# A graph layer's projection dealt out between the tiles of its sums, and counts with one column of weights

## The chip, the cores and the metric

The kernel runs on one core of a Trainium2 chip. The metric is device time in microseconds (us) from launch to end; runs of one kernel agree within about 0.3%. The core's engines are TensorE (PE in the profile, with its weight loads as PEld), VectorE (DVE), ScalarE (ACT), GpSimd (POOL) and SyncE (SP); they run their own instruction streams and wait for one another by semaphores.

## The reference

Two graph convolutions over 6,250 nodes of 256 features and 100,000 edges in eight relations, then a mixture of experts. The edges come sorted by their target dst, and the density of targets falls with dst. Cut to what matters:

```python
def _rgcn_conv(x, W, Wroot, b, src, dst, etype):
    xs = x[src]
    seg = dst * R + etype
    sums = jax.ops.segment_sum(xs, seg, num_segments=N * R)
    cnt = jax.ops.segment_sum(jnp.ones_like(xs[:, 0]), seg, num_segments=N * R)
    mean = sums / jnp.maximum(cnt, 1.0)[:, None]
    mean = mean.reshape(N, R, -1)
    return x @ Wroot + b + jnp.einsum('nrd,rde->ne', mean, W)

h = relu(_rgcn_conv(layernorm(x), W1, Wroot1, b1, src, dst, etype))
x = x + _rgcn_conv(h, W2, Wroot2, b2, src, dst, etype)
# then 8 experts, the best 2 per node: x + sum_e w_e (gelu(ln(x) @ W1[e] + b1[e]) @ W2[e] + b2[e])
```

## The kernel before

Preparation (to about 118 us) normalises x and writes it to DRAM as three bf16 parts per value, whose sum is the f32 value (xs). Then the function `layer` runs twice (the two convolutions), and then the expert stage.

The 100,000 edges are 782 *tiles* of 128 edges. `_plan` joins neighbouring tiles into 194 *groups* of one to six tiles, so that all targets of a group lie in a window of at most 64 nodes. It deals the groups out in one sequence, `seq`, from both ends of the edge list towards a block near the middle; one group is one *step* q. The nodes are 49 *blocks* of 128. `whole[b]` is the step after whose group no edge of block b is left, by an estimate with a margin `dev` (L167).

For a group, `tiles_in` (L668) does three things. ACT writes zeros into a window of sums `pg` in PSUM (L672; two buffers, so a group's zeros wait for the sum of the group two before it to be taken out). GpSimd issues one indirect DMA per tile, which fetches the 128 source rows into a buffer `ge` (L680, 13 buffers). DVE makes a one-hot matrix `oh` per tile (L686). `sums` (L691) then runs on TensorE: per tile six matmuls with the gathered rows as weights (two halves of the features by three bf16 parts) and `oh` as the moving operand (L696); in layer 0 a seventh with a 128 x 128 matrix of ones as weights (L699), which counts the edges into the third slice of `pg`. `add` (L702) lets DVE add the window to a ring in SBUF that holds the sums of three blocks (L710); there are two rings, for the two ends.

When a block is whole, a few functions finish it. `counts` (L751) fetches the counts of its nodes by an SP DMA from partition 0 of the ring (cn, L760), `invert` (L763) transposes them and takes reciprocals. `project` (L770) runs nine products on TensorE, the node's own features with Wroot and the eight relations' sums with W (L783: 36 passes of 256 columns in f32), two at a time into a PSUM buffer `pr` (two buffers), and DVE gathers them into `h` with the reciprocals (L791, L793). `clear` (L797) lets ACT zero the block's slots in the ring (L800). `finish` (L803) writes the block's rows to DRAM, by SP; in layer 0 after relu and a split into three bf16 parts (L808 to L815), in layer 1 with a layernorm besides. `turn` (L824) transposes the block on TensorE for its next use (L830, L314). `logits` (L835) works out the gate of the experts, and for every few blocks picks the experts (`choose`) and appends the nodes to the experts' lists (`append`, one block per step, eight SP DMAs, L423).

The table `due` (L848) says how many steps after `whole[b]` each of them is emitted: root -1, counts 0, invert 1, project, clear and finish 2, turn 3, logits 4. In step q the loop (L866) emits the next group's `tiles_in`, then project and clear, turn, finish, then this group's `sums`, invert and logits, then `add`, root and counts. A scheduler then sets the final order on each engine from the dependencies and its own costs, so that the emitted order is a wish. Engines issue in that final order.

Ring slots are shared, so `_plan` also gives each group `bounds` (L171 to L177): the first and last block that its window may touch. They are worked out from the steps at which blocks are read (`read`, with READ = 2) and cleared (`taken`, with TAKE = 3), and are checked against the data on the chip before the layers run; data that break them take another, slower path. Adds and projections have no semaphores between them where the bounds part them; an add waits for the clears that are due before its step.

Of the kernel before, what the change touches and what calls it, by code (L numbers as in the profile page):

```python
# [48 lines left out]
P = 128  # L49
# [45 lines left out]
Z = 4.8  # L95
WIN = 64
RB = 3
READ = 2
TAKE = 3
EARLY = 30  # L100

# [1 line left out]
def _plan(N, E, R):  # L103

    T = -(-E // P)

    def windows(ts, n):

        mid = n // 2
        lo, hi = [0] * n, [-(1 << 30)] * n
        for t in ts:
            for k in range(n + 1):
                i0, i1 = t * P, max(0, t + k - mid) * P
                mean = N * (i1 * i1 - i0 * i0) / (E * E)
                sd = 2 * N * i0 / (E * E) * math.sqrt(abs(i1 - i0)) + 0.004 * abs(mean)
                if k < n:
                    lo[k] = min(lo[k] if t != ts[0] else 1 << 30, math.floor(mean - Z * sd) - (k < mid))
                if k:  # L120
                    hi[k - 1] = max(hi[k - 1], math.ceil(mean + Z * sd) + (1 if k <= mid else 2))
        shift = -min(lo)
        w = [(a + shift, b + shift) for a, b in zip(lo, hi)]
        return shift, w, max(b for _, b in w)


    NB = -(-N // P)
    mid = max(0, round((N / 4 - P / 2) / P))
    split = round(T * math.sqrt((mid + 0.5) * P / N))
    regions = []  # L130
    t = 0
    while t < T:
        left = (split if t < split else T) - t
        for n in range(min(6, left), 0, -1):
            ng = max(1, min(36, left) // n)
            shift, w, width = windows((t + n // 2, t + n * (ng - 1) + n // 2), n)
            if width <= WIN:
                break
        regions.append((t, n, ng, shift, w, width))
        t += n * ng  # L140
    groups = []
    for r, (t0, n, ng, *_) in enumerate(regions):
        for g in range(ng):
            groups.append((t0 + g * n, n, r))
    NG = len(groups)
    up = [g for g in range(NG) if groups[g][0] < split]
    down = list(range(NG - 1, len(up) - 1, -1))
    size = [sum(groups[g][1] for g in s) for s in (up, down)]
    seq, at, n = [], [0, 0], [0, 0]
    while len(seq) < NG:  # L150

        s = int(n[1] * (size[0] - EARLY) < n[0] * size[1])
        if at[s] == len((up, down)[s]):
            s = 1 - s
        g = (up, down)[s][at[s]]
        seq.append(g)
        at[s] += 1
        n[s] += groups[g][1]
    step = {g: q for q, g in enumerate(seq)}

    whole = []
    for b in range(NB):
        if b == mid:
            whole.append(NG - 1)
            continue
        p = math.sqrt((b + 1 if b < mid else b) * P / N)
        dev = Z * math.sqrt(E * p * (1 - p)) + 1  # L167
        t = int(min(E - 1, E * p + dev) // P) if b < mid else int((E * p - dev) // P)
        whole.append(step[next(g for g, (t0, n, _) in enumerate(groups) if t0 + n > t)])


    bounds = []
    for g in range(NG):
        read, taken = ([b for b in range(NB) if whole[b] + n < step[g]] for n in (READ - 1, TAKE))
        if g < len(up):
            bounds.append((sum(b < mid for b in read) or -NB, sum(b < mid for b in taken) + RB))
        else:  # L177
            n = sum(b > mid for b in read)
            bounds.append((NB - sum(b > mid for b in taken) - RB, NB - n if n else 2 * NB))
    return T, regions, groups, seq, len(up), mid, whole, bounds  # L180
# [3 lines left out]
def kernel(  # L184
# [20 lines left out]
    nc = tc.nc  # L205
    N, D = x.shape
    E = src.shape[0]
    R = gW1.shape[0]
    X = fW1.shape[0]
    H = fW1.shape[2]  # L210
    KD = D // P
    KH = H // P
    NB = -(-N // P)
# [28 lines left out]
    ones16 = const.tile([P, P], BF16, name="ones16")  # L242
# [84 lines left out]
    T, regions, groups, seq, UP, mid, whole, bounds = _plan(N, E, R)  # L327
    assert T == C
    NG = len(groups)
# [306 lines left out]
    with tc.If(go == 1) as cmp:  # L636
        with ExitStack() as arm:
# [9 lines left out]
            step = {g: q for q, g in enumerate(seq)}  # L647
# [8 lines left out]
            def layer(k):  # L656
# [34 lines left out]
                def sums(g):  # L691
                    pg, got = state[g]
                    for ge, oh, m, a, b in got:
                        for c in range(KD):
                            for s in range(3):
                                nc.tensor.matmul(pg[:, c, :, a:b], ge[:m, s, c, :], oh, start=False, stop=False,  # L696
                                                 skip_group_check=True)
                        if nd > KD:
                            nc.tensor.matmul(pg[:, KD, :, a:b], ones16[:m], oh, start=False, stop=False,  # L699
                                             skip_group_check=True)  # L700

                def add(g):  # L702
                    pg, _ = state.pop(g)
# [59 lines left out]
                def invert(b):  # L763
                    if k == 0:
# [2 lines left out]
                        nc.vector.tensor_scalar(invs[:, b], pc[:, :R], 1.0, None, op0=OP.max)  # L767
                        nc.vector.reciprocal(invs[:, b], invs[:, b])

                def project(b):  # L770

                    n = rows(b)
                    xT = state.pop(("x", b))
                    s0 = (b % RB) * P
                    ring = of(b)
                    h = ap.tile([P, D], F32, name="h", bufs=2)
                    lhs = [(R, [xT[:, c, :n] for c in range(KD)])]
                    lhs += [(r, [ring[:, c, r, s0 : s0 + n] for c in range(KD)]) for r in range(R)]
                    for i in range(0, R + 1, 2):
                        pr = psum.tile([P, 2, D], F32, name="pr", tag="mm", bufs=MM)  # L780
                        for j, (r, chunks) in enumerate(lhs[i : i + 2]):
                            for c in range(KD):
                                mm = nc.tensor.matmul(pr[:n, j], chunks[c], w[:, c, r, :], start=(c == 0), stop=(c == KD - 1))  # L783
                                if r < R:
                                    for a in adds[int(b > mid)][state["adds", b] :]:
                                        tc.declare_no_dep(of_block(b, mm), a, reason="bounds")
                                    tc.add_manual_dep(mm.ins, state["whole", b].name, wait, reason="whole")
                        for j, (r, _) in enumerate(lhs[i : i + 2]):
                            if r == R:
                                extra = bias1 if k == 0 else state.pop(("xb", b))  # L790
                                nc.vector.tensor_tensor(h[:n], pr[:n, j], extra[:n], OP.add)  # L791
                            else:
                                nc.vector.scalar_tensor_tensor(h[:n], pr[:n, j], invs[:n, b, r : r + 1], h[:n],  # L793
                                                               op0=OP.mult, op1=OP.add)
                    state["h", b] = h

                def clear(b):  # L797
# [47 lines left out]
                tiles_in(seq[0])  # L845
                due = {}
                for b, q in enumerate(whole):
                    for d, f in ((-1, root), (0, counts), (1, invert), (2, project), (2, clear), (2, finish), (3, turn), (4, logits)):  # L848
                        due.setdefault(q + d, []).append((f, b))

                todo = []
# [8 lines left out]
                def run(q, *fs):  # L860
                    for f, b in due.get(q, []):
                        if f in fs:
                            f(b)

                cleared[:] = [[(-1, ins) for _, ins in c] for c in cleared]
                for q in range(NG + 5):  # L866
                    if k == 1 and q == 2:

                        with tc.issue_after(state["zeroed"].ins):
                            load_gnn_weights(gW2, None, None, nc.scalar, gw)  # L870
                    batch()
                    if q + 1 < NG:
                        tiles_in(seq[q + 1])
                    if q == 0 and k == 0:
                        for c in range(KD + 1):
                            nc.vector.memset(rings[0][:, c], 0.0)
                            nc.scalar.copy(rings[1][:, c], zeros[:, None, 0:1].to_broadcast([P, R, RING + WIN]))
                    run(q, project, clear)
                    run(q, turn)
                    run(q, finish)  # L880
                    if q < NG:
                        sums(seq[q])
                    run(q, invert, logits)
                    if q < NG:
                        add(seq[q])
                    run(q, root, counts, join)
# [6 lines left out]
    with cmp.Else():  # L893
        with ExitStack() as arm:
# [35 lines left out]
            with tc.tile_pool(name="sortp", bufs=1, side="right") as sp:  # L930
# [22 lines left out]
                for d in range(NB):  # L953
                    oh = sp.tile([P, C], F32, name="oh", bufs=2)
# [319 lines left out]
```

## Time and profile before

| | |
|---|---|
| median of 10 runs | 3026.54 us (3020.66 to 3031.13) |
| the profiled execution | 3027.49 us, span 3025.7 us |
| mean granted TensorE clock | 0.927 |
| gathers of layer 0, first to last start | 81.9 to 1121.2 us |
| gathers of layer 1, first to last start | 1162.2 to 2160.6 us |
| expert stage's first weight DMA | 2219.2 us |
| DVE ring adds, L710 | x388, 1176 ns, 456.3 us |
| ACT zeroing of pg, L672 | x388, 981 ns, 380.0 us |
| ACT clearing of the ring, L800 | x98, 2325 ns, 227.8 us |

A row of the profile names line, engine, operation, output and inputs, the count, then busy time, mean ns of one, and the idle time of the engine just before, with what ended it. In rows in order of time, the first number is the start in us from the span's start, the second the time in us. A stretch's row has its length, then the busy time of PE, PEld, DVE, ACT and POOL with the number of instructions, then the granted clock, the DMA share and GB/s. A wait's row has the total in us, how often, and the longest. Matmuls are pipelined: an instruction's duration (240 ns) is its latency, and successors start far closer.

### The profile page before, as it was taken

To read this page: it belongs to the slowest core of one execution; us is meant where nothing else is said; L and a number is where in the kernel's file an instruction comes from. 1 tells how busy PE (TensorE), PEld (TensorE's weight loads), DVE (VectorE), ACT (ScalarE), POOL (GpSimd) and SP (SyncE) were. 2 spreads that over 40 slices of the span, in tenths; PEclk is the share of its full clock that TensorE was granted. 3 is DMA by queue.
4 is the path that set the end of the run, shared out by engine and by line. 5 is a ranking of instruction groups with operands and counts; after the bars stand their busy time and mean duration, and the time that the engine had idled before them with its cause. 6 is when DMAs were issued, how large, how long until landed. Compare 5 with 4: busy or idle time off the path is not lost.

```text
span 3025.7 us, 52037 instructions
## 1 busy us (share of the span) xinstructions
PE 2553.5 (84%) x18131; PEld 2157.9 (71%) x18131; DVE 1620.6 (54%) x4676; ACT 1018.8 (34%) x1378; POOL 1811.2 (60%) x2109
## 2 busy tenths in 40 slices
PE   5578888888888876888888888898839999999997
PEld 2466776776777765666766767777728888888886
DVE  7566676766666674666766776676711111111111
ACT  6334444434343442333323323233312222222221
POOL 1767777777777764777777777777413333333332
PEclk9789999999999997989989998999969999999999
DMA  7555565656555554666566666666364444444441
GB/s 259 149 144 161 166 173 164 173 157 170 162 171 165 167 142 132 176 176 176 169 174 176 174 177 169 175 180 173 111 200 117 109 117 107 108 122 107 107 120 20
DMA packets 215591, 461.05 MB, mean 152 GB/s; under 512 B 50716, under 2 KB 123222, under 8 KB 215190
## 3 DMA queue, kind: packets, MB, share of 16 engines
q0 software_dynamic: 120384, 334.45, 41.6%
q1 hardware_dynamic: 83724, 112.33, 11.2%
q10 hardware_dynamic: 11210, 10.81, 1.2%
q8 instruction: 149, 2.44, 0.3%
q14 instruction: 124, 1.02, 0.1%
HBM read 412.02 MB, written 46.31 MB: 151 GB/s over the span
## 4 chain that ended last, share of the span: by engine, by line
PE 63%; DMA 20%; ACT 5%; DVE 5%; issue 4%; POOL 1%; SPq 0%; DVEq 0%; ACTq 0%; POOLq 0%
PE pr L783 25%; DMA ge<-xs,idx 15%; PE ph L1214 12%; PE po L1225 12%; PE pg L696 11%; ACT ring L800 2%; DVE ring L710 2%; ACT pg L672 1%; DMA cn<-ring 1%; POOL ge L680 1%; DMA xt<-in_x_dram 1%; ACT xt L496 1%; PE pt L1198 1%; PE pg L699 1%; DMA fw<-in_L_ffn_W_dram 1%
## 5 line engine op out<-in xcount | busy, mean ns | idle before, releaser
L680 POOL DMA_INDIRECT ge<-xs,idx x1564 | 1522.0, 973 | 622.1 <-issue 224.4
L696 PE MATMUL pg<-oh,ge 128*128 128x200 bf16 (+24 forms) x9384 | 827.1, 240 | 321.5 <-DMA ge<-xs,idx 227.4
L696 PEld LDWEIGHTS <-ge 128*128 128x128 bf16 x9384 | 669.8, 104 | 443.6 <-DMA ge<-xs,idx 279.9
L783 PE MATMUL pr<-gw,ring 128*128 128x256 f32 (+1 forms) x3136 | 753.0, 395 | 2.1 <-DVE h L793 1.8
L783 PEld LDWEIGHTS pr<-gw,ring 128*128 128x128 f32 (+1 forms) x3136 | 615.9, 199 | 99.0 <-DVE h L793 5.8
L710 DVE TENSOR_TENSOR ring<-pg,ring 128x1176 f32 (+31 forms) x388 | 456.3, 1176 | 279.4 <-PE pg L696 136.1
L672 ACT COPY pg<-zeros 128x1176 f32<-128x1176 f32 (+31 forms) x388 | 380.0, 981 | 528.0 <-DVE ring L710 505.3
L793 DVE SCALAR_TENSOR_TENSOR h<-pr,invs,h 128x256 f32<-128x256 f32 (+1 forms) x784 | 376.4, 480 | 165.4 <-PE pr L783 148.5
L800 ACT COPY ring<-zeros 128x3072 f32<-128x3072 f32 (+1 forms) x98 | 227.8, 2325 | 686.1 <-PE pr L783 625.5
L1215 ACT ACTIVATE hT<-ph,bcol 128x256 f32<-128x256 f32 x424 | 200.8, 474 | 534.5 <-PE ph L1214 534.5
L1214 PE MATMUL ph<-xT,w 128*128 128x256 f32 x1696 | 378.3, 382 | 0.0
L1225 PE MATMUL po<-fw,hT 128*128 x1696 | 374.4, 379 | 0.0
L1225 PEld LDWEIGHTS po<-fw,hT 128*128 128x128 f32 x1696 | 322.2, 190 | 43.8
L1214 PEld LDWEIGHTS ph<-xT,w 128*128 128x128 f32 x1696 | 321.0, 192 | 42.2
L686 DVE TENSOR_SCALAR oh<-iota,rel 128x152 bf16<-128x152 f16 (+25 forms) x1564 | 335.4, 274 | 19.6 <-PE pg L699 14.6
L1186 POOL DMA_INDIRECT xg<-xnd,ti x106 | 105.6, 996 | 350.0 <-DMA ti<-tlist 236.0
L1230 POOL DMA_INDIRECT out_dram<-fo,ti x106 | 168.7, 1591 | 230.2 <-DVE wt L1199 116.3
L1228 DVE TENSOR_TENSOR fo<-po,b2b 128x256 f32<-128x256 f32 x106 | 45.0, 425 | 299.4 <-PE po L1225 299.4
L699 PE MATMUL pg<-oh,ones 128*128 128x128 bf16 (+24 forms) x782 | 187.8, 240 | 0.0
L1209 DVE COPY bcol<-b1c 128x8 f32 x53 | 9.0, 171 | 302.4 <-ACT hT L1215 301.9
L699 PEld LDWEIGHTS <-ones 128*128 128x128 bf16 x782 | 82.3, 105 | 2.6
L783 PE MATMUL pr<-gw,hTs 128*128 128x256 f32 (+1 forms) x196 | 70.9, 485 | 2.3 <-ACT hTs L831 2.1
(190 smaller groups left out, 1345.2 us busy)
## 6 DMA issues: line engine op xcount, KB each, us to landing
w<-in_L_ffn_W_dram SPq DMA_DIRECT2D x53, 1024.0 KB
ge<-xs,idx POOLq DMA_INDIRECT x1564
xt<-in_x_dram SPq DMA_DIRECT2D x96, 128.0 KB
xs<-xb SPq DMA_DIRECT2D x8, 1152.0 KB
xs<-hb SPq DMA_DIRECT2D x48, 192.0 KB
fw<-in_L_ffn_W_dram ACTq DMA_DIRECT2D x8, 1024.0 KB
xt<-in_x_dram SPq DMA_DIRECT2D x8, 768.0 KB
out_dram<-h SPq DMA_DIRECT2D x48, 128.0 KB
```

Of the source, the lines that this page charges most:

```text
L672: state["zeroed"] = nc.scalar.copy(pg[:, :nd, :, :wd], zeros[:, None, None, :wd].to_broadcast([P, nd, R, wd]))
L680: nc.gpsimd.indirect_dma_start(out=ge[:m].rearrange("p s k d -> p (s k d)"), out_offset=None, in_=xs[k][:, :], in_offset=bass.IndirectOffs ...
L686: nc.vector.tensor_scalar(oh, iota16[:m].rearrange("p (r d) -> p r d", r=R)[:, :, a:b], rel[:m, t : t + 1], None, op0=OP.is_equal)
L696: nc.tensor.matmul(pg[:, c, :, a:b], ge[:m, s, c, :], oh, start=False, stop=False, skip_group_check=True)
L699: nc.tensor.matmul(pg[:, KD, :, a:b], ones16[:m], oh, start=False, stop=False, skip_group_check=True)
L710: a = nc.vector.tensor_tensor(slot, pg[:, :nd, :, :wd], slot, OP.add).ins
L783: mm = nc.tensor.matmul(pr[:n, j], chunks[c], w[:, c, r, :], start=(c == 0), stop=(c == KD - 1))
L793: nc.vector.scalar_tensor_tensor(h[:n], pr[:n, j], invs[:n, b, r : r + 1], h[:n], op0=OP.mult, op1=OP.add)
L800: ins = nc.scalar.copy(at, zeros[:, None, None, 0:1].to_broadcast([P, nd, R, P]))
L1214: nc.tensor.matmul(ph[:, :TK], w1[:, k, h * P : (h + 1) * P], xT[:, k, :], start=(k == 0), stop=(k == KD - 1))
L1215: nc.scalar.activation(hT[:, h, :], ph[:, :TK], AF.Gelu, bias=bcol[:, h : h + 1], scale=1.0)
L1225: nc.tensor.matmul(po[:, :D], hT[:, k, f * P : (f + 1) * P], rhs, start=(k == 0), stop=(k == KH - 1))
```

## The change

`project` no longer issues its nine products. It makes a function `pair` for each two of them and puts them into a list, `pairs`. `sums` takes one from the list after each tile (`go_on`), and what is left follows the group's last tile. Within a step, turn and clear now come first, then finish, project, `sums` with the pairs, the leftover pairs, and the rest as before. Clear, finish, turn and logits are due one step later, and there is one step more at the end. The counts matmul loads one column of the ones and writes partition 0 alone; the other partitions of the third slice keep the zeros. `READ` is gone, `read` is worked out without the extra step, and the margin `dev` grows from 1 to 32 edges.

```diff
-        dev = Z * math.sqrt(E * p * (1 - p)) + 1
+        dev = Z * math.sqrt(E * p * (1 - p)) + P / 4
...
-        read, taken = ([b for b in range(NB) if whole[b] + n < step[g]] for n in (READ - 1, TAKE))
+        read, taken = ([b for b in range(NB) if whole[b] + n < step[g]] for n in (0, TAKE))
...
-                            nc.tensor.matmul(pg[:, KD, :, a:b], ones16[:m], oh, start=False, stop=False,
+                            nc.tensor.matmul(pg[0:1, KD, :, a:b], ones16[:m, 0:1], oh, start=False, stop=False,
                                              skip_group_check=True)
+                        go_on()
...
+                pairs = []
+
+                def go_on():
+
+                    if pairs:
+                        f, i = pairs.pop(0)
+                        f(i)
...
-                    for i in range(0, R + 1, 2):
+                    def pair(i):
                         pr = psum.tile([P, 2, D], F32, name="pr", tag="mm", bufs=MM)
...
+                    pairs.extend((pair, i) for i in range(0, R + 1, 2))
                     state["h", b] = h
...
-                    for d, f in ((-1, root), (0, counts), (1, invert), (2, project), (2, clear), (2, finish), (3, turn), (4, logits)):
+                    for d, f in ((-1, root), (0, counts), (1, invert), (2, project), (3, clear), (3, finish), (4, turn), (5, logits)):
...
-                for q in range(NG + 5):
+                for q in range(NG + 6):
...
-                    run(q, project, clear)
-                    run(q, turn)
+                    run(q, turn, clear)
                     run(q, finish)
+                    run(q, project)
                     if q < NG:
                         sums(seq[q])
+                    while pairs:
+                        go_on()
```

More of the change, by code (lines that the diff above doesn't have):

```diff
@@ L97 @@
 RB = 3
-READ = 2
 TAKE = 3
```

## The prediction

> **What bounds the kernel now.** I read the page's engine sums first, then the costliest groups, then GpSimd's rows in order of time, then TensorE's waits.
>
> The page's engines and groups:
>
> ```profile
> span 3025.7 us, 52037 instructions
> ...
> PE 2553.5 (84%) x18131; PEld 2157.9 (71%) x18131; DVE 1620.6 (54%) x4676; ACT 1018.8 (34%) x1378; POOL 1811.2 (60%) x2109
> ...
> L680 POOL DMA_INDIRECT ge<-xs,idx x1564 | 1522.0, 973 | 622.1 <-issue 224.4
> L696 PE MATMUL pg<-oh,ge 128*128 128x200 bf16 (+24 forms) x9384 | 827.1, 240 | 321.5 <-DMA ge<-xs,idx 227.4
> ...
> L783 PE MATMUL pr<-gw,ring 128*128 128x256 f32 (+1 forms) x3136 | 753.0, 395 | 2.1 <-DVE h L793 1.8
> ...
> L699 PE MATMUL pg<-oh,ones 128*128 128x128 bf16 (+24 forms) x782 | 187.8, 240 | 0.0
> ```
>
> POOL's 60% hides a saturated engine, because the expert stage (from 2219 us on) hardly uses it. GpSimd's rows in order of time show it:
>
> ```profile
> 652.75 0.95 POOL L680 DMA_INDIRECT ge<-xs,idx  x1 [0.30 <-issue]
> 654.00 0.94 POOL L680 DMA_INDIRECT ge<-xs,idx  x1 [0.30 <-issue]
> ...
> 660.80 0.95 POOL L680 DMA_INDIRECT ge<-xs,idx  x1 [5.86 <-PE pg L696]
> 662.05 0.94 POOL L680 DMA_INDIRECT ge<-xs,idx  x1 [0.30 <-PE pt L830]
> ```
>
> Each gather is followed by 0.30 us whatever the releaser named; 1,541 of the 1,563 gaps are 0.3 us. Gathers run from 81.9 to 1122.2 us in layer 0 and from 1162.2 to 2161.6 in layer 1. What the longer gaps have over 0.31 us sums to 34 us in layer 0 and 7 in layer 1; the one at the layer change is 40. So issuing alone needs 1040 - 34 = 1006 us in layer 0 (1.29 per tile) and 992 in layer 1. Nothing that only helps TensorE can win more than the 41 us in which GpSimd waited for one of 13 buffers. TensorE over layer 0's sums (88 to 1129 us), by stretch and by waits:
>
> ```profile
> 88.00:1129.00 1041.00, 861.35 (x7389) 737.41 (x7385) 702.76 (x1669) 435.31 (x481) 762.98 (x778) 0.92 0.58 163
> ...
> PE pg L696 <- DMA ge<-xs,idx: 80.4, 103, 3.9
> PE pg L696 <- ACT pg L672: 66.7, 62, 5.6
> PE pt L830 <- DVE h L808: 15.9, 13, 3.9
> PE pc L766 <- DMA cn<-ring: 10.1, 14, 2.1
> ```
>
> TensorE is second in line: 861 us busy. About 207 busy stretches end in a wait, and each counts a matmul's tail (0.24 long, while its successor would start 0.07 after it): 35 us. Its own need is 826. The parts agree: 782 tiles at 0.48 (the mean of 471 undisturbed cycles of seven matmuls) are 375, 49 blocks of 36 projection passes at 0.231 are 408, transposes about 40.
>
> **The counts (L699).** One matmul per tile of layer 0, 782 of them, keeps its moving columns and loads one weight column instead of 128. Before, it costs only its streaming: L696 to L699 to L696 runs without a break (1126.00, next at 1126.07). Narrow weights do occur in this trace: L411 loads eight columns, L383 one. L411 between the same sums:
>
> ```profile
> 1541.99 0.22 PE L411 MATMUL rpl<-rcol,rnum 128*8 128x128 bf16 x1
> 1542.14 0.34 PE L696 MATMUL pg<-oh,ge 128*128 128x176 bf16 x2
> 1542.41 0.22 PE L411 MATMUL rpl<-rcol,rnum 128*8 128x128 bf16 x1
> ...
> 1543.73 0.22 PE L411 MATMUL rpl<-rcol,rnum 128*8 128x128 bf16 x1
> 1543.88 0.25 PE L696 MATMUL pg<-oh,ge 128*128 128x176 bf16 x1
> 1544.06 0.22 PE L411 MATMUL rpl<-rcol,rnum 128*8 128x128 bf16 x1
> ```
>
> From L411 to L411 with one 176-column matmul between is 0.33 us; streamed at the usual pace (0.057 for L411's 128 columns, 0.078 for 176) it would be 0.135. With two between: 0.42 against 0.21. So a narrow matmul costs about 0.20 us more: its load isn't started under the matmul ahead, nor the next wide load under it. For one column, L381 to L383 takes 0.11 where L380 to L381 takes 0.03, and the second L383 to the next sum about 0.10: some 0.16 more. The load rows read 80 ns for one column and about 100 for 128. Bounds: -0.02 x 782 = -16 us, if only the load's duration mattered, to 0.25 x 782 = 196. I take 0.18, between the two measured forms, since L383 has the weights and L411 the length and the neighbours of the new count: **+141 us of TensorE in layer 0**, none in layer 1 (no counts there).
>
> The Trainium skill ("TensorE: Matmul & The Clock Gate", LDWEIGHTS) has load time grow with the number of columns; by that alone one column saves nearly 0.1 us of loading per tile, and by estimate 83 us of loads would go. The same page's "Weight-path perf modes" reserves its fast load for exactly 128 columns of a type other than FP32, which speaks against this change. The rows of L383 and L411 side with the second: loads barely shorter, and a gap on both sides.
>
> **The projection dealt out (L779 to 796, pairs run from `sums`).** The 36 passes and eight DVE accumulations of a block stay the same. Emitted whole, a project of 36 passes holds TensorE about 8 us while GpSimd issues 6 gathers; the 5.86 us stall above follows two projects 4 us apart. Afterwards each tile's buffer comes free at least as early. The compiled order of the changed kernel keeps part of the lumps: of 882 projection matmuls per layer, those in runs of 16 or more without a tile between fall from 484 to 194 (layer 0) and from 531 to 140 (layer 1). Switching costs a little: the load of an f32 pass is 0.19 us and a bf16 matmul ahead hides half of it, so 0.1 each; runs of projection rise from 86 to 137 in layer 0 (+5 us) and from 93 to 189 in layer 1 (+10, in idle time). A run behind a narrow count pays 0.09 more (L411, two f32 passes, L411: 0.78 us against 0.49, less the 0.20): 137 x 0.09 = +12.
>
> **Clear, finish, turn and logits a step later; bounds.** Clear (L800, 2.3 us on ACT, 98 times) no longer sits in ACT's queue behind a project; it waited 625 us there, which cost TensorE little. Turn comes a step after finish, so the 16 us of TensorE waiting for L808 go. Clear stands nearer to the add that needs its slots (DVE waited 6.7 us for it in 10 cases); if every block waits 1 us, 98 us of DVE queue, which is hidden while buffers are free. The SP DMAs of finish are the same in number, a step later, and nobody reads them before the layer ends. I worked the plan's new bounds through with the reference's dst: the ring arm is still the one taken. The wider `dev` moves two of 49 blocks by one group. NG + 6 steps add one empty step.
>
> **Tail.** The compiled order puts the three-block choice behind the next-to-last project, so at the end one more list append comes after the last project. An append cycle is 4.6 to 5.2 us (L415 at 2199.40, 2204.60, DVE free at 2209.2); it partly overlaps: **+2**, between 0 and +5. The gap at the layer change stays: the same adds, cn DMA and two projects; 0.
>
> **Sum.** Layer 0, TensorE: 826 + 141 + 5 + 12 = 984 us of own need, against GpSimd's 1006. With the servers this close, the waits decide. ACT's zeroing (62 times, 1.08 us and 0.17 of tail) shrinks as a three-tile group now takes 0.6 us longer: 62 x 0.65 = 40. cn stays: 12. Of the waits for gathers (103 x 0.95 = 98) I keep a quarter, since a queue of 13 buffers between equal servers still runs dry at the start and after stalls: 25. 984 + 77 = 1061 against 1041: **+20**. Layer 1: TensorE keeps its slack, of 7 us of stall 5 go: **-5**. Tail **+2**. Total +17 on the profiled execution's 3027.49, which stands 0.95 above the median of the ten: 3043.5, say **3044 us**.
>
> **Rivals.**
> - *Smoothing wins.* If a count costs under about 0.1 us more, TensorE's need stays below 930 and GpSimd's stalls mostly go: -34 and -5 of them at best, less what is left of early stalls (14 us by 240 us, at a granted clock of 0.85): about 3000, at the very best 2988. For it: buffers do come free earlier, layer 1's lumps shrink most, and a TensorE that idles less may hold a higher granted clock (0.92 over layer 0; f32 passes average 0.231 us, 0.216 undisturbed), worth up to 0.06 x 826 = 50 us of need. Against it: the L411 rows. The sign flips where 826 + 17 + 77 + 782 times the count's extra comes to 1044 (1041 and the 3 us that layer 1 and the tail give back): at 0.16 us, which is the value of the one-column rows; below it the kernel is faster.
> - *Nothing measurable (within 0.2%, 6 us, about what a measurement of this kernel can tell).* Counts between 0.15 and 0.17 us extra, or a clock gain that pays for dearer ones.
> - *Much slower.* Counts at 0.25 (+55) with ACT's waits unshrunk (+37, because clear now falls between the zeroings): 3044 + 55 + 37 = 3136, or 3081 to 3099 with one of them.
>
> **Numbers.** Slower by TensorE's need 0.56 (much slower within that: 0.12), nothing 0.14, faster 0.30. Range 2999 to 3092: it leaves out the best of the smoothing case and the far end of the much slower one. Within the forecast's own case: 3033 to 3092.
>
> **What would show it.** Gaps of about 0.1 us on both sides of each count, tile cycles of about 0.65 in place of 0.48; TensorE busy near 95% in layer 0 with its waits for gathers down from 80 us to some 25; GpSimd's long gaps (PE pg) growing in layer 0 to over 50 us and almost none in layer 1; the wait for L808 gone. The forecast is wrong if tile cycles stay near 0.5, or if TensorE's clock rises enough to pay for the counts.

## The result, and the profile after

The changed kernel takes 3055.74 us (median of 11 runs, 3039.96 to 3063.01), the kernel before 3023.87 (39 runs, 3013.04 to 3033.20). The ratio is 1.0103, with an interval of 1.0090 to 1.0116: slower by 32 us or 1.0%, where 17 us were forecast. The profiled execution took 3058.49 us, its span is 3056.7, 31.0 more than before. By the starts of GpSimd's gathers, these 31 us lie as follows:

| us | before | after | difference |
|---|---|---|---|
| up to the first gather | 81.9 | 83.4 | +1.6 |
| layer 0, first to last gather | 1039.3 | 1068.6 | +29.3 |
| of it, gaps of GpSimd beyond 0.31 us | 34.4 | 65.8 | +31.4 |
| layer change, last to first gather | 41.0 | 41.2 | +0.2 |
| layer 1, first to last gather | 998.4 | 994.4 | -4.0 |
| of it, gaps beyond 0.31 us | 7.2 | 2.5 | -4.8 |
| after the last gather | 865.1 | 869.0 | +3.9 |

So the loss is layer 0's, the only layer that counts edges, and there it is time that GpSimd waits for a buffer. The page of the changed kernel, its engines and groups:

```profile
span 3056.7 us, 52032 instructions
...
PE 2674.8 (88%) x18131; PEld 2151.1 (70%) x18131; DVE 1618.0 (53%) x4676; ACT 1015.3 (33%) x1378; POOL 1809.4 (59%) x2110
...
L679 POOL DMA_INDIRECT ge<-xs,idx x1564 | 1520.5, 972 | 650.7 <-PE pg L695 231.7
L695 PE MATMUL pg<-oh,ge 128*128 128x200 bf16 (+24 forms) x9384 | 907.2, 243 | 238.7 <-DMA ge<-xs,idx 143.6
...
L791 PE MATMUL pr<-gw,ring 128*128 128x256 f32 (+1 forms) x3136 | 766.8, 392 | 2.7 <-DVE h L801 2.7
...
L698 PE MATMUL pg<-oh,ones 128*1 128x128 bf16 (+24 forms) x782 | 180.9, 231 | 0.0
...
L698 PEld LDWEIGHTS <-ones 128*1 128x1 bf16 x782 | 62.1, 79 | 107.0 <-issue 58.8
```

The counts' own row (L698) looks cheaper than before, 180.9 us against 187.8, and their load takes 79 ns. TensorE's sum is 121 us higher all the same. The largest part of GpSimd's idle time (231.7 of 650.7 us, which include the 0.30 us behind every gather) is now put down to `PE pg L695`, the matmuls that free a gather's buffer. Where the 121 us come from is seen only in TensorE's rows in order of time. Here are the same tiles at the full clock, 192 and 272 columns wide, first in the kernel before, then in the changed kernel:

```profile
308.33 0.66 PE L696 MATMUL pg<-oh,ge 128*128 128x192 bf16 x6
308.83 0.25 PE L699 MATMUL pg<-oh,ones 128*128 128x192 bf16 x1
308.91 0.70 PE L696 MATMUL pg<-oh,ge 128*128 128x192 bf16 x6
309.44 0.26 PE L699 MATMUL pg<-oh,ones 128*128 128x192 bf16 x1
309.53 0.86 PE L696 MATMUL pg<-oh,ge 128*128 128x272 bf16 x6
```

```profile
329.22 0.67 PE L695 MATMUL pg<-oh,ge 128*128 128x192 bf16 x6
329.82 0.24 PE L698 MATMUL pg<-oh,ones 128*1 128x192 bf16 x1
330.00 0.71 PE L695 MATMUL pg<-oh,ge 128*128 128x192 bf16 x6
330.64 0.25 PE L698 MATMUL pg<-oh,ones 128*1 128x192 bf16 x1
330.82 0.87 PE L695 MATMUL pg<-oh,ge 128*128 128x272 bf16 x6
```

From one tile's first sum to the next tile's it was 0.58 and 0.62 us, and is 0.78 and 0.82. Over 521 cycles of seven matmuls without a gap above 0.15 us the mean is 0.674 us, over 494 such cycles before it was 0.479; this mixes widths and granted clocks. At one width (medians) the extra is nearly the same everywhere: 0.19 at 24 columns, 0.20 at 152, 0.20 at 256. About half of it lies behind the count (0.16 us to the next sum in place of 0.08) and half ahead of it. At 0.19 us, 782 of these make 149 us. The two stretches of the changed kernel (layer 0's sums, layer 1's) and TensorE's waits in layer 0:

```profile
88.00:1160.00 1072.00, 979.77 (x7380) 729.49 (x7380) 704.17 (x1665) 434.19 (x477) 761.96 (x779) 0.93 0.56 158
1193.00:2190.00 997.00, 835.44 (x6739) 691.03 (x6740) 665.54 (x2177) 298.17 (x364) 754.89 (x782) 0.91 0.62 176
```

```profile
PE pg L695 <- ACT pg L671: 57.2, 56, 5.4
PE pg L695 <- DMA ge<-xs,idx: 34.9, 25, 16.1
PE pc L766 <- DMA cn<-ring: 10.4, 15, 1.8
PE pt L839 <- DVE h L817: 2.0, 3, 1.0
```

The longest wait for a gather, 16.1 us, is the one ahead of the layer's first matmul. It stood in the kernel before as well, where it ended ahead of the window of the waits, which starts at 88 us (before, then after):

```profile
86.64 0.32 PE L696 MATMUL pg<-oh,ge 128*128 128x40 bf16 x4 [16.12 <-DMA ge<-xs,idx]
```

```profile
88.20 0.28 PE L695 MATMUL pg<-oh,ge 128*128 128x40 bf16 x3 [16.13 <-DMA ge<-xs,idx]
```

TensorE is busy 980 of 1072 us (91%, 83% before). Without that first one, its waits for gathers fell from 80 us in 103 cases to 19 us in 24, the wait for `h` from 16 to 2; the wait for ACT's zeros only from 67 to 57. GpSimd shows the other side:

```profile
490.74 0.94 POOL L679 DMA_INDIRECT ge<-xs,idx  x1 [1.76 <-PE pg L695]
491.99 0.94 POOL L679 DMA_INDIRECT ge<-xs,idx  x1 [0.30 <-issue]
499.30 0.94 POOL L679 DMA_INDIRECT ge<-xs,idx  x1 [6.37 <-PE pg L695]
500.54 0.94 POOL L679 DMA_INDIRECT ge<-xs,idx  x1 [0.30 <-PE pg L695]
```

Gaps over 0.33 us grew from 17 to 42 in layer 0 and fell from 4 to 2 in layer 1. Of their 66 us 52 lie before 500 us, where 17 of 34 lay in the kernel before: all of the loss. From 88 to 400 us the granted clock fell, though TensorE was busier. The stretches from 200 to 300 and from 300 to 400 us, before and after:

```profile
200.00:300.00 100.00, 83.70 (x723) 72.55 (x724) 67.49 (x172) 41.56 (x48) 73.18 (x77) 0.91 0.58 164
300.00:400.00 100.00, 80.83 (x752) 69.90 (x750) 67.89 (x162) 45.00 (x50) 74.98 (x79) 0.93 0.60 168
```

```profile
200.00:300.00 100.00, 86.45 (x625) 63.53 (x624) 63.27 (x149) 38.04 (x43) 63.29 (x65) 0.85 0.49 138
300.00:400.00 100.00, 90.63 (x671) 65.66 (x670) 60.63 (x150) 35.82 (x39) 70.19 (x73) 0.88 0.56 158
```

The clock's record knows two values in this layer, 1.0 and 0.5. Of these 200 us, 31 ran at 0.5 before and 53 after, and at 0.5 a tile's cycle of 200 columns takes 1.21 us before and 1.41 after (medians of 3 and 9), where GpSimd issues a gather every 1.25 us. How much of the loss comes by way of the clock is not shown.

### The profile page after: what moved, and what is told of

Same layout as the page of the kernel before. It is cut to its first block, busy times and chain, and to the rows that moved or that the text cites. A ratio compares the mean times of both kernels' runs of the same rounds, so it can differ in the third digit from the quotient of the medians.

```text
span 3056.7 us, 52032 instructions
## 1 busy us (share of the span) xinstructions
PE 2674.8 (88%) x18131; PEld 2151.1 (70%) x18131; DVE 1618.0 (53%) x4676; ACT 1015.3 (33%) x1378; POOL 1809.4 (59%) x2110
## 4 chain that ended last, share of the span: by engine, by line
PE 70%; DMA 14%; ACT 5%; DVE 5%; issue 4%; POOL 1%; SPq 0%; DVEq 0%; ACTq 0%; POOLq 0%
PE pr L791 25%; PE pg L695 15%; PE ph L1225 12%; PE po L1236 12%; DMA ge<-xs,idx 9%; PE pg L698 3%; DVE ring L710 2%; ACT pg L671 2%; ACT ring L809 1%; POOL ge L679 1%; DMA xt<-in_x_dram 1%; DMA cn<-ring 1%; PE pt L1209 1%; PE pt L313 1%; PE pl L322 1%
## 5 line engine op out<-in xcount | busy, mean ns | idle before, releaser
L679 POOL DMA_INDIRECT ge<-xs,idx x1564 | 1520.5, 972 | 650.7 <-PE pg L695 231.7
L695 PE MATMUL pg<-oh,ge 128*128 128x200 bf16 (+24 forms) x9384 | 907.2, 243 | 238.7 <-DMA ge<-xs,idx 143.6
L695 PEld LDWEIGHTS <-ge 128*128 128x128 bf16 x9384 | 664.9, 105 | 399.0 <-DMA ge<-xs,idx 175.2
L791 PE MATMUL pr<-gw,ring 128*128 128x256 f32 (+1 forms) x3136 | 766.8, 392 | 2.7 <-DVE h L801 2.7
L791 PEld LDWEIGHTS pr<-gw,ring 128*128 128x128 f32 (+1 forms) x3136 | 591.8, 195 | 87.2 <-DVE h L801 4.3
L710 DVE TENSOR_TENSOR ring<-pg,ring 128x1464 f32 (+30 forms) x388 | 456.6, 1177 | 284.6 <-PE pg L695 128.1
L698 PE MATMUL pg<-oh,ones 128*1 128x128 bf16 (+24 forms) x782 | 180.9, 231 | 0.0
L698 PEld LDWEIGHTS <-ones 128*1 128x1 bf16 x782 | 62.1, 79 | 107.0 <-issue 58.8
L315 ACT COPY tT<-pt 128x256 f32<-128x256 f32 (+1 forms) x98 | 36.2, 370 | 147.1 <-PE pt L313 129.8
```

The lines of the kernel that those rows point to most:

```text
L679: nc.gpsimd.indirect_dma_start(out=ge[:m].rearrange("p s k d -> p (s k d)"), out_offset=None, in_=xs[k][:, :], in_offset=bass.IndirectOffs ...
L698: nc.tensor.matmul(pg[0:1, KD, :, a:b], ones16[:m, 0:1], oh, start=False, stop=False, skip_group_check=True)
L710: a = nc.vector.tensor_tensor(slot, pg[:, :nd, :, :wd], slot, OP.add).ins
```

## The experiments

The theory: the dealt-out order takes lumps away and costs nothing; the narrow counts cost TensorE 0.19 us each; and in layer 0, where TensorE and GpSimd are nearly level, part of that comes back as waits of GpSimd. The rival: the order itself costs (dealt-out pairs, later steps), and the counts are hidden.

The chips were not alike: on the two that the first eleven runs fell on the kernel before takes 3793 to 3833 us, on that of the last run 3024, and every ratio is to the kernel before beside it on the same chip.

| run | kernel | us | kernel before there | ratio |
|---|---|---|---|---|
| e1_wide_counts | dealt out, counts of 128 columns | 3697.66 | 3832.76 | 0.9643 (0.9604 to 0.9681) |
| e2_narrow_only | kernel before, narrow counts | 3838.41 | 3832.76 | 0.9998 (0.9971 to 1.0024) |
| e3_wide_undealt | later steps, not dealt out, 128 columns | 3834.63 | 3832.76 | 1.0006 (0.9988 to 1.0024) |
| e4_counts_last | dealt out, narrow counts in one run per group | 3703.51 | 3832.76 | 0.9669 (0.9629 to 0.9709) |
| r2_changed | the changed kernel | 3671.54 | 3793.36 | 0.9680 (0.9645 to 0.9714) |
| r2_wide_counts | as e1 | 3668.36 | 3793.36 | 0.9667 (0.9642 to 0.9693) |
| r2_narrow_only | as e2 | 3803.02 | 3793.36 | 1.0021 (1.0002 to 1.0040) |
| l1_light_before | kernel before, a third of the gathered bytes | 3827.94 | 3798.28 | 1.0085 (1.0053 to 1.0117) |
| l2_light_changed | changed kernel, a third of the gathered bytes | 3713.04 | 3798.28 | 0.9793 (0.9753 to 0.9833) |
| l3_light_wide | as e1, a third of the gathered bytes | 3700.42 | 3798.28 | 0.9746 (0.9714 to 0.9778) |
| r3_wide_counts | as e1 | 3660.45 | 3798.28 | 0.9632 (0.9603 to 0.9661) |
| n1_counts_twice | the changed kernel, each narrow count twice | 3186.29 | 3023.75 | 1.0541 (1.0517 to 1.0565) |

### One part at a time

Wide counts in the changed kernel:

```diff
-                            nc.tensor.matmul(pg[0:1, KD, :, a:b], ones16[:m, 0:1], oh, start=False, stop=False,
+                            nc.tensor.matmul(pg[:, KD, :, a:b], ones16[:m], oh, start=False, stop=False,
```

> The changed kernel with the counts' weights 128 columns wide again; the order on every engine stays that of the changed kernel. Theory (the narrow load costs 0.19 us per tile and makes TensorE a second bound of layer 0): the tile cycle returns from 0.63 to 0.45 us at the median, GpSimd's waits for buffers in layer 0 fall from 66 us to under 20, the time to about 3000 us (2990 to 3012), faster than before. Rival (the order is what costs: pairs between tiles, clear and finish a step later): within 12 us of the changed kernel, 3044 or more.

The same lines the other way round in the kernel before (narrow counts alone):

> The kernel before with the counts' weights one column wide, and nothing else. Theory: TensorE needs some 145 us more in layer 0, and with whole projects of 8 us GpSimd waits for buffers more than the 66 us of the changed kernel: 3060 to 3090 us. Rival (the order is what costs): 3024 us, like the kernel before.

Wide counts, and the changed kernel's list of pairs emptied where `project` stands, so that only the later steps and bounds of the change are left:

```diff
                     run(q, project)
+                    while pairs:
+                        go_on()
                     if q < NG:
                         sums(seq[q])
```

> Wide counts, and each block's five pairs issued together ahead of the group's sums; clear, finish, turn and logits stay a step later. Theory (buffers come free earlier because pairs stand between tiles): most of the gain of the wide dealt kernel is missing, 3010 to 3026 us, and GpSimd still waits over 25 us in layer 0. Rival (ACT's and TensorE's waits were the cause, and the later clear and turn are what helps): within 6 us of the dealt kernel with wide counts.

Narrow counts, all of a group's in one run behind its sums:

```diff
+                        go_on()
+                    for ge, oh, m, a, b in got:
                         if nd > KD:
                             nc.tensor.matmul(pg[0:1, KD, :, a:b], ones16[:m, 0:1], oh, start=False, stop=False,
                                              skip_group_check=True)
-                        go_on()
```

> The changed kernel with its one-column counts issued in one run at the end of each group, 196 runs instead of 782. Theory (what costs is the change between narrow and wide weights, once per run): 196 x 0.19 = 37 us of TensorE instead of 149, GpSimd's waits in layer 0 under 30 us, 3000 to 3018 us. Rival (each narrow matmul costs by itself, by its load or by its write to one partition): as the changed kernel, 3045 to 3060 us.

Measured: 0.9643, 0.9998, 1.0006 and 0.9669. On this chip dealing the pairs out gains all of 3.3 to 3.6%; later steps and bounds alone (e3) and narrow counts alone (e2) do nothing that can be told from zero. Two expectations missed. One is the level: the kernel before took 3833 us there, so no forecast in microseconds holds. The other is the theory's for e2, which was to be 1.012 to 1.022 of the kernel before and is 0.9998, as its rival had it. A gain larger than all of GpSimd's waits in the first profile (41 us) could only come from waits that the first profile doesn't have, so the changed kernel itself had to be run on such a chip.

### The changed kernel on a slower chip

No edit: the changed kernel, and e1 and e2 again.

> The changed kernel once more, as the reference point of this call. Where gathers land as fast as in the first profiles (kernel before about 3024 us), 1.010 of the kernel before. Where the kernel before takes about 3830 us and most of TensorE's waiting is for late gathers, dealing out should win whatever the counts cost: 0.965 to 0.975.

> Wide counts, dealt out. Theory (narrow counts cost TensorE 149 us in layer 0, and that matters where GpSimd's issue is the only other bound): where the kernel before takes about 3024 us, 0.988 to 0.996 of it, with GpSimd's waits for buffers in layer 0 under 20 us and a tile cycle of 0.45 us at the median. Rival (the order is what costs): within 0.4% of the changed kernel. Where the kernel before takes 3830 us, 0.964 again.

> The kernel before with narrow counts only. Theory: where the kernel before takes about 3024 us, 1.012 to 1.025 of it, with GpSimd's waits in layer 0 over 66 us, because whole projects and dearer tiles add up. Rival (counts are harmless): 1.000. Where the kernel before takes 3830 us, 1.000 again.

All three are near what was expected for a chip of this kind: 0.9680 (0.965 to 0.975), 0.9667 (0.964) and 1.0021 (1.000). The change that costs 1.0% on the first chip gains 3.2% here. The stretches of layer 0 and layer 1 tell why the counts don't matter here. First the changed kernel, then the one with wide counts:

```profile
88.00:1430.00 1342.00, 1065.62 (x7271) 768.49 (x7272) 691.42 (x1645) 431.15 (x472) 748.44 (x775) 0.84 0.44 126
1490.00:2780.00 1290.00, 904.62 (x6582) 735.63 (x6582) 652.01 (x2132) 294.38 (x357) 735.05 (x766) 0.83 0.47 133
```

```profile
88.00:1430.00 1342.00, 959.27 (x7239) 794.89 (x7240) 687.98 (x1639) 428.45 (x470) 754.84 (x775) 0.82 0.44 125
1490.00:2780.00 1290.00, 900.89 (x6573) 729.83 (x6570) 651.78 (x2132) 294.25 (x357) 737.87 (x766) 0.83 0.47 133
```

Narrow counts add 106 us of busy TensorE in layer 0 and nothing in layer 1 (904.6 and 900.9). Layer 0 ends at the same place, its last gather at 1432.6 and 1434.8 us. With 71% busy there was room for them. GpSimd waits 356 and 351 us in layer 0 here, where the first profile had 34, and 323 and 322 in layer 1, where it had 7; and it is these waits that dealing out shortens: e3 to e1, both with wide counts on one chip, from 407 to 371 in layer 0 and from 420 to 335 in layer 1.

What the narrow count costs is the change of width, and not the width. In e4 (count at its L700), on the chip of e1, layer 0's stretch has 960.8 us of busy TensorE against e1's 950.9:

```profile
88.00:1430.00 1342.00, 960.81 (x7152) 752.73 (x7150) 674.51 (x1610) 421.38 (x463) 738.12 (x763) 0.83 0.43 124
```

```profile
88.00:1430.00 1342.00, 950.92 (x7179) 789.91 (x7177) 681.67 (x1620) 423.95 (x466) 739.98 (x765) 0.82 0.43 124
```

Ten us in place of 106; the expectation had 37, for 196 runs of counts at 0.19, and the trace has 196 runs, 70 of them with a wait behind them that can hide half of the cost. In a row the counts follow one another as wide ones do; e4's rows:

```profile
919.86 1.49 PE L695 MATMUL pg<-oh,ge 128*128 128x112 bf16 x27
921.28 0.46 PE L700 MATMUL pg<-oh,ones 128*1 128x128 bf16 x6
921.68 0.44 PE L313 MATMUL pt<-ident,xt 128*128 128x128 f32 x2
```

Six counts take 0.40 us to the next instruction's start, where six alternating ones pay 6 x 0.19 on top of their streaming.

### Is it the gathered bytes that make these chips slow?

In three kernels (before, changed, and changed with wide counts) a gather fetches 512 bytes per row in place of 1536; the two lower parts of the features are left out:

```diff
-    xs = [dram.tile([N, S3], BF16, name=f"xs{k}") for k in range(2)]
+    xs = [dram.tile([N, D], BF16, name=f"xs{k}") for k in range(2)]
...
-                            out=ge[:m].rearrange("p s k d -> p (s k d)"), out_offset=None, in_=xs[k][:, :],
+                            out=ge[:m, 0].rearrange("p k d -> p (k d)"), out_offset=None, in_=xs[k][:, :],
...
-                                nc.tensor.matmul(pg[:, c, :, a:b], ge[:m, s, c, :], oh, start=False, stop=False,
+                                nc.tensor.matmul(pg[:, c, :, a:b], ge[:m, 0, c, :], oh, start=False, stop=False,
```

> The kernel before with light gathers: a gathered row is the first of its three bf16 parts alone (512 bytes instead of 1536), and the three matmuls of a sum all read that part; the features are kept in one part too, so that two thirds of what the gathers and the stores of features move, and the two lower parts of the features, are left out. Instructions of TensorE, VectorE and ScalarE stay the same in number and size. On the chips of the last runs the kernel before takes 3793 to 3833 us in place of 3024, with GpSimd waiting for buffers some 350 us in each layer. If it is the bytes of the gathers that come late there, this kernel takes about 3020 us on such a chip (2980 to 3060), and TensorE is again busy over 80% of layer 0. If instructions come late on all engines, whatever the gathers move, it stays within 3% of the kernel before beside it.

> The changed kernel with the same light gathers (two thirds of the gathered bytes and the two lower parts of the features left out). Theory: where the gathers aren't late, TensorE has little slack in layer 0 and the narrow counts' 0.19 us each (149 us) come back as waits of GpSimd: this takes 1.008 to 1.013 of the light kernel before, as the full kernels did at first (1.0103). If the light kernels are still slow (near 3800 us), it is 0.96 to 0.97 of the light kernel before, as on the chips of the last runs.

> The changed kernel with counts of 128 columns and the light gathers (two thirds of the gathered bytes and the two lower parts of the features left out): the dealt-out order alone. Theory: where the gathers aren't late, the order takes lumps away and costs nothing, so 0.985 to 0.997 of the light kernel before, and 40 to 70 us below the light changed kernel. Rival: it is the order that costs (dealt-out pairs and the later steps), and the narrow counts are hidden: then it is within 10 us of the light changed kernel, 1.007 to 1.013 of the light one before.

> The changed kernel with counts of 128 columns, full gathers, on another draw of a chip. On a chip where the kernel before takes about 3024 us: 2985 to 3018 us (0.985 to 0.998 of it) if the narrow counts are what cost the changed kernel its time; 3045 to 3060 us if the order is. On a chip where the kernel before takes about 3800 us: 0.964 to 0.967 of it once more.

It isn't: with a third of the bytes the kernel before takes 1.0085 of its time, and GpSimd still waits 397 and 394 us in the two layers. That guess fell. The changed kernel and the one with wide counts stand as on such chips before (0.9793 and 0.9746 of the kernel before, 0.970 and 0.967 of the light one, 3713.04 and 3700.42 over 3827.94), and e1 once more gives 0.9632 (0.964 to 0.967 was expected). So these runs didn't bring back the first chip's regime, and said nothing on the sign there.

### Double the suspected cost

```diff
                         for c in range(KD):
                             for s in range(3):
                                 nc.tensor.matmul(pg[:, c, :, a:b], ge[:m, s, c, :], oh, start=False, stop=False,
                                                  skip_group_check=True)
-                        if nd > KD:
-                            nc.tensor.matmul(pg[0:1, KD, :, a:b], ones16[:m, 0:1], oh, start=False, stop=False,
-                                             skip_group_check=True)
+                            if nd > KD:
+                                nc.tensor.matmul(pg[0:1, KD, :, a:b], ones16[:m, 0:1], oh, start=False, stop=False,
+                                                 skip_group_check=True)
```

> The changed kernel with its one-column count issued twice in every tile, after the first half of the sums and after the second, so that each of the two stands between loads of 128 columns (every edge is counted twice and the means come out halved). By the trace of the changed kernel one more such count costs TensorE 0.19 us for the switch and about 0.07 us for itself, 782 of them some 200 us in layer 0; layer 1 has no counts and must stay as it is. Theory: what a count costs in the end depends on the slack TensorE has left. Where the kernel before takes about 3800 us, TensorE is busy 1066 of layer 0's 1342 us in the changed kernel and 959 with wide counts, and these 107 us cost nothing; with 200 more it is nearly full, and 40 to 110 us of them must show: 0.978 to 0.998 of the kernel before. Where the kernel before takes about 3024 us, nearly all of them show: 1.05 to 1.08. Rival: the counts are free whatever they take (only the order matters): within 10 us of the changed kernel, 0.965 to 0.971 on the slow chips, 1.010 on the other.

This run fell on a chip where the kernel before takes 3023.75 us, and gave 1.0541: the theory's 1.05 to 1.08, not the rival's 1.010. Against the changed kernel's 3055.74 (1.0103) it is 131 us. Layer 0's and layer 1's stretches, then TensorE's waits in layer 0:

```profile
88.00:1272.00 1184.00, 1149.23 (x8088) 753.69 (x8088) 701.72 (x1654) 435.16 (x474) 759.24 (x778) 0.95 0.50 143
1314.00:2311.00 997.00, 837.80 (x6749) 693.33 (x6750) 667.49 (x2180) 298.33 (x364) 749.37 (x782) 0.90 0.61 176
```

```profile
PE pg L695 <- ACT pg L671: 25.4, 15, 4.1
PE pc L766 <- DMA cn<-ring: 2.8, 4, 1.1
...
PE pg L695 <- DMA ge<-xs,idx: 2.1, 4, 0.7
```

At the full clock the second count makes a tile's cycle longer by 0.20 us at 24 columns, 0.24 at 112 and 0.31 at 256 (medians), its own streaming included. TensorE is now 97% busy in layer 0: it is the bound there. Layer 0's last gather moved from 1152.1 to 1264.5 us (+112), GpSimd's long gaps there from 66 to 181 us. The layer change grew by 9 us, layer 1, which has no counts, stayed (990.3 us from first to last gather, 994.4 in the changed kernel), and the stretch after the last gather has 3 more: 120 us of span between the two profiled executions.

The three kernels of this kind of chip make a row for layer 0: busy 861, 980 and 1149 us; not busy 180, 92 and 35; stretch 1041, 1072 and 1184. The first step of 118 us of TensorE, which came with the new order, lengthened the layer by 31; the next, of 169 us with nothing else changed, by 112. Time put on the second engine in line is paid first out of its own waits, and the fewer of these are left, the more of it shows.

What was not run is e1, the dealt-out order with wide counts, on a chip of the first kind. So the version that ought to be best, e1 or e4, is shown only to beat the kernel before on the slower chips (by 3.3 to 3.7%), not to beat the changed kernel there (0.9667 and 0.9680, overlapping intervals), and nothing of it is shown on the first kind. That the order alone costs nothing there has one row for it: layer 1 of the changed kernel is dealt out too, has no counts, and is 4 us shorter. So the counts' cost on TensorE is measured, and that such a cost lengthens layer 0 on this kind of chip is shown by the last run; that all 31 us are theirs, and none the order's in layer 0, is argued.

## Why the prediction was right, and where it was short

**The count's extra.** Taken as 0.18 us, between two narrow matmuls that the trace of before happened to hold (about 0.16 and 0.20); measured 0.19, 149 us in place of 141. The mechanism, a gap on both sides of the count, is the one that was forecast. The Trainium skill ("TensorE: Matmul & The Clock Gate", LDWEIGHTS) lets load time fall with the columns; the load did fall, from 105 to 79 ns, and TensorE got 118 us busier all the same. The measurement decides. By the same page's "Weight-path perf modes" a fast load is for 128 columns of a type other than FP32, so a narrow one goes without; e4's row, six narrow counts in 0.40 us, shows that this alone costs next to nothing here, and the change of width costs.

**TensorE's own need in layer 0.** Forecast 984 us. Measured: 979.8 busy, less a tail of 0.17 us for each of the 99 waits shown (17), is 963. It was too high by 21. The term of 12 for narrow counts ahead of f32 passes isn't there: in the changed kernel's trace, at the full clock, a pass starts as soon behind a count as a sum does behind a count of the same width (the median difference of 74 is under 0.01 us). What makes up the rest is not shown; the mean clock of the layer, 0.93 in place of 0.92, is worth some 10 us by estimate (a hundredth of 963).

**The waits that stay: the term that was mis-sized.** Forecast 77 us (ACT 40, cn 12, gathers 25); measured 1072 - 963 = 109. With 0.17 us of tail for each, and without the first wait of the layer, which lies ahead of the stretch, the measured parts are ACT 67, cn 13, gathers 23 and 6 of small ones that the sum had at nothing. So the keeping of a quarter of the gathers' waits was right, and the term that failed is the wait for ACT's zeros: I let it shrink from 1.08 to 0.48 us each, because a group's tiles now take longer. It stayed at 57.2 us in 56 waits, 1.02 each, and fell, to 25 us, only in the run with twice the counts. In 25 of these 56 (24.2 us; 24 and 18.6 us before) the zeroing had itself waited, with ACT idle, for DVE's add that frees one of the two windows; in most of the others ACT was busy with something else. Why longer tiles did not shorten them is open. Need 21 too high and waits 32 too low make the 11 us by which layer 0 was under-forecast (+31 against +20): two misses of opposite sign, so the sum came nearer than its parts.

**Layer 1 and tail.** Layer 1: -5 forecast, -4.0 measured. Tail: +2 forecast, +3.9 measured. The start, which the forecast had at nothing, is +1.6.

**Rivals.** The smoothing rival was right in its mechanism for layer 1, and for the whole kernel on chips where GpSimd waits over 300 us in a layer. Its flip point on the first chip, 0.16 us per count, was passed by the measured 0.19. The much slower rival was right that ACT's waits do not shrink, but not in its reason, that clear falls between the zeroings: waits for a zeroing that stood behind a clear fell from 12.1 us to 1.5. The prediction knew one chip, and its sign holds only for that kind of chip.

**What it said would show.** Cycles of 0.65: 0.674. GpSimd's gaps over 50 us in layer 0 and almost none in layer 1: 65.8 and 2.5. TensorE's waits for gathers down to some 25 us: 19, besides the layer's first. The wait for `h` gone: 15.9 to 2.0. TensorE at 95%: 91, because its need was lower and more waits stayed.

## What to carry to other kernels

A smaller operand isn't a cheaper one: in this kernel a narrow weight between wide ones costs 0.19 us each time, and the row of the instruction itself shows a saving; read its cost from start to start of its neighbours, and keep narrow matmuls together if they are wanted. Cost on an engine that is not the bound is first taken out of that engine's waits, so add up need and waits of the stretch, and treat waits for another engine's preparation (here ACT's zeros) as staying until a row shows that they shrink. When two engines are nearly level, the sign of a change can hang on the chip that the run falls on: compare on more than one.

## What was not expected of the hardware

One program differs by a quarter between chips. The kernel before takes 3024 us beside the first runs and beside the last one, and 3793 to 3833 beside the others. The stretch after the last gather hardly differs (869 us in the changed kernel's first profile, 876 in r2_changed), GpSimd's gather takes 0.97 and 0.96 us, and issuing 782 of them at 1.27 to 1.29 us, as the first profile has it, needs some 1000 us of the 1310 to 1350 that a layer takes there. The profile also names other ends of the waits. The shares of the chain that ended last, for the kernel before on the first chip and then for r2_wide_counts:

```profile
PE 63%; DMA 20%; ACT 5%; DVE 5%; issue 4%; POOL 1%; SPq 0%; DVEq 0%; ACTq 0%; POOLq 0%
```

```profile
PE 59%; issue 13%; DVE 10%; another core or an unknown queue 8%; ACT 5%; DMA 4%; POOL 0%; ACTq 0%; SPq 0%; DVEq 0%; POOLq 0%
```

"Issue" is time in which an engine waits for nothing that the profile shows. In layer 0 of r2_wide_counts TensorE waits that way, too:

```profile
PE pg L695 <- issue: 91.9, 114, 3.6
PE pr L791 <- issue: 42.2, 17, 11.1
```

On the first chip no such row stands among TensorE's waits. But the traces of the slower chips are not whole: r2_changed holds 25,843 semaphore updates where the same program's first trace holds 48,202, with the same 52,032 instructions. What is missing is missing in the two layers (6 and 8 updates a us, against 17 and 22 on the first chip) and hardly in the last stretch (8 against 9), which is also the stretch that isn't slower. So an "issue" there may be no more than a wait whose end wasn't recorded, and who ends the waits can't be compared. It isn't the gathered bytes (l1). Whether it is the chip that is slower, or the recording that holds it up there, no run here tells: every run listed for these chips carries a recorded span and clock.

The mean granted clock of layer 0 was 0.92 at 83% busy, 0.93 at 91%, 0.95 at 97%; on the slower chips it was 0.82 at 71% and 0.84 at 79%. The rows from 200 to 400 us above run the other way, so a rule doesn't follow from these means. Part of an added load may pay for itself by the clock: the second count of each tile should have cost some 200 us (782 times 0.19 and 0.07), and TensorE's busy time grew by 169. Some 13 of the 31 us are tails, by estimate (0.17 us each for 104 waits that became 29); that the clock pays for the rest is not shown.
